# Row maxima moved by DMAs inside SBUF, and causal masking of exponentials on GpSimd

## The chip, the core and the metric

The kernel runs on one core of a Trainium2 chip. The metric is the device time in microseconds (us) of one execution; the number for a kernel is the median of several runs. An execution is also recorded by the hardware profiler, instruction by instruction. The engines are named as the profile names them: PE is the matrix engine (PEld its weight loads), DVE the vector engine, ACT the scalar engine, POOL GpSimd, and SP the engine that here only issues DMAs. PE writes into PSUM, which has eight banks of 512 fp32 columns on each of the 128 partitions; DVE and ACT read PSUM, and POOL in this kernel reads and writes SBUF only.

## The reference, cut to what matters

The reference is a stack of eight gated layers over x (4 batches, 256 tokens, 256 features). The change lies in one of them, the cross-attention of layer 1: 16 heads of 16 features, queries from the normalized x, keys and values from a context of 64 features, and a causal mask. Per batch and head it computes

```
q = (layernorm(x) @ Wq.T), k and v from ctx @ Wkv_expand.T     # 256 x 16 each
scores = (q @ k.T) / sqrt(16), where key index > query index: masked out
attn = softmax(scores, axis=-1)
out = (attn @ v), heads side by side, @ Wout.T
x = x + tanh(g_xattn[1]) * out
```

A softmax is not changed if any constant is taken off all scores of one query. The kernel takes off the maximum of that query's unmasked scores, so that the exponentials stay in range.

## The kernel before, in words

**Layout.** Queries and keys lie transposed: features on partitions, tokens along the row. The sixteen heads are handled in four quadruples j = 0..3; in one quadruple, head n = 0..3 has the 32 partitions 32n to 32n+31, of which 16 are features. Partition 32n+16 (`D1` within the group) is one more row: in the keys tile `kT` it holds 1.0, in the queries tile `qT` it starts as zero. Whatever is written into that row of `qT` is added to every score of that query, so the negated maximum is put there. The 256 x 256 scores of one head have three 128 x 128 blocks that are not wholly masked: two on the diagonal (blocks 0 and 2) and one below it (block 1). They fill 384 columns of a PSUM bank.

**Two passes over the scores.** `Maxima.score(j)` computes the scores with queries on the partitions (lines 945 and 950), reduces each block's row maximum on DVE (line 956), and joins the two blocks of the second half of the queries (lines 961, 962). `Maxima.late(j)`, one round later, turns these columns into rows with two PE transposes (line 968) and DVE adds the transposed 128 x 256 tile to the queries of quadruple j (line 971). For that the maxima are put into column 16 of each 32-wide group of a zeroed tile (`cms`). `Sums.score(j)` then computes the same scores with keys on the partitions (lines 985 and 990), now with the maximum taken off, and ACT takes the exponential of each head's 384 columns (line 996) into the SBUF tile `pT`. `Sums.sum(j)`, one round later, multiplies `pT` with the values (lines 1004 and 1009); a column of ones in the values gives the softmax's denominators.

**The mask** is added by PE: in both passes `masked(side)` first multiplies an identity with a constant tile `cmask` that has -1e30 at the masked places of the two diagonal blocks (line 919, four products of 256 columns, one for each head's bank), and the scores are accumulated on top. `side` chooses the orientation.

**The order of work.** Within this stage the order of PE, DVE, ACT and POOL instructions is the order in which the program gives them; DMAs of SP, and work of later stages, are placed by the scheduler. The stage is a loop of rounds n = 0, 1, 2, ... (line 1071), four for each of the four batches. In round n the quadruple n mod 4 of batch b = n div 4 goes through `Maxima.score`, then the products of the round before (`Sums.sum`), then `Sums.score` for the same quadruple of batch b-1, then one to three steps of an unrelated top-k on DVE (`graph_rows`, lines 511 to 518), then the late parts: `Maxima.late`, `Sums.late` (every second round, PE transposes of line 1025 and DVE work), a turn of the attention output (line 1041), its product with the output weights, and in rounds 1, 5 and 9 the query projection of the next batch (both line 237). Maxima run in rounds 0 to 15, Sums in rounds 4 to 19. All PSUM tiles take one of eight banks in turn: four for a `Maxima.score`, four for a `Sums.score`, one for the accumulated products over two rounds, one for each late transpose.

Of the kernel before, what the change touches and what calls it, by code (L numbers as in the profile page):

```python
# [18 lines left out]
F32 = mybir.dt.float32  # L19
BF16 = mybir.dt.bfloat16  # L20
U32 = mybir.dt.uint32
AF = mybir.ActivationFunctionType
ALU = mybir.AluOpType
AX = mybir.AxisListType
# [3 lines left out]
P = 128  # L28
B, S, D, C = 4, 256, 256, 64
# [5 lines left out]
H1, D1 = 16, 16  # L35
# [8 lines left out]
NEG = -1.0e30  # L44
# [24 lines left out]
def flamingo(ctx: ExitStack, tc: tile.TileContext, a: dict, out: bass.AP):  # L69
    nc = tc.nc  # L70

    const = ctx.enter_context(tc.tile_pool(name="const", bufs=1))
# [18 lines left out]
    def bank(dtype=F32):  # L91
        return pools[1].tile([P, 512 if dtype == F32 else 1024], dtype, tag="b1", name="b1")
# [72 lines left out]
    ident = const.tile([P, P], F32, tag="ident", name="ident")  # L165
# [461 lines left out]
    with tc.tile_pool(name="l0a", bufs=1) as lp:  # L627
        tiles0 = normalized(0, *statistics(0))
        pk = bank()
        for i in range(2):  # L630
            nc.tensor.matmul(
                pk[half(i), :], cw[half(i), CW_KV0 : CW_KV0 + C], ctxT[half(i)].rearrange("c h s -> c (h s)"),
                start=True, stop=True,
            )
        pn = [bank()[:, : 4 * C].rearrange("p (t c) -> p t c", t=4) for _ in range(2)]
# [134 lines left out]
    onesb = const.tile([P, P], BF16, tag="onesb", name="onesb")  # L770
    nc.gpsimd.memset(onesb, 1.0)


    cmask = const.tile([P, 2, 3, P], BF16, tag="cmask", name="cmask")
    nc.gpsimd.memset(cmask, 0.0)
    for side, sign in ((0, -1), (1, 1)):
        for blk in (0, 2):
            nc.gpsimd.affine_select(
                out=cmask[:, side, blk, :], in_=cmask[:, side, blk, :], pattern=[[sign, P]],
                compare_op=ALU.is_ge, fill=NEG, base=0, channel_multiplier=-sign,  # L780
            )

    rows_in = tc.dram_tile([NB * P, D], F32, name="rows_in")
    rows_out = tc.dram_tile([NB * P, D], F32, name="rows_out")
# [4 lines left out]
        out=before, in_=onesb, pattern=[[1, P]], compare_op=ALU.is_ge, fill=0.0, base=-1, channel_multiplier=-1  # L789
# [4 lines left out]
        out=lower, in_=lower, pattern=[[1, E], [-1, E]], compare_op=ALU.is_ge, fill=0.0, base=-1,  # L794
        channel_multiplier=0,
# [102 lines left out]

    with ExitStack():
        lp = l1a
        wo = weights(a["l1_wo"], KC * D)
        nc.sync.dma_start(
            rows_in.rearrange("(n p) d -> p n d", p=P), zero.unsqueeze(1).to_broadcast([P, NB, D])
        )
        cms = []
        for n in range(2):
            cm = lp.tile([P, 2, 4, 32], F32, tag=f"cm1_{n}", name=f"cm1_{n}", bufs=1)
            nc.gpsimd.memset(cm, 0.0)  # L910
            cms.append(cm)
        def group(n):
            return slice(32 * n, 32 * (n + 1))

        def masked(side):

            pn = [bank() for _ in range(4)]
            for n in range(4):
                nc.tensor.matmul(
                    pn[n][:, : 3 * P].rearrange("p (a k) -> p a k", a=3)[:, 0::2, :], identb,  # L920
                    cmask[:, side, 0::2, :], start=True, stop=False,
                )
            return pn

        class Maxima:
# [14 lines left out]

            def score(self, j):
                b, qT = self.b, self.qT
                pn = masked(0)
                for n in range(4):
                    nc.tensor.matmul(
                        pn[n][:, :P], qT[group(n), j, :P], kT[group(n), j, b * S : b * S + P],
                        start=False, stop=True,
                    )
                for n in range(4):
                    nc.tensor.matmul(  # L950
                        pn[n][:, P : 3 * P], qT[group(n), j, P:], kT[group(n), j, b * S : (b + 1) * S],
                        start=False, stop=True, skip_group_check=True,
                    )
                m3 = lp.tile([P, 4, 3], F32, tag="m31", name="m31")
                for n in range(4):
                    nc.vector.tensor_reduce(  # L956
                        m3[:, n, :], pn[n][:, : 3 * P].rearrange("p (a k) -> p a k", a=3), AX.X, ALU.max,
                        negate=True,
                    )
                cm = cms[j % 2]  # L960
                nc.vector.tensor_copy(cm[:, 0, :, D1], m3[:, :, 0])
                nc.vector.tensor_tensor(cm[:, 1, :, D1], m3[:, :, 1], m3[:, :, 2], ALU.min)

            def late(self, j):

                pt = bank()[:, :S]
                for qt in range(2):
                    nc.tensor.transpose(
                        pt[:, qt * P : (qt + 1) * P], cms[j % 2][:, qt].rearrange("p g c -> p (g c)"), ident
                    )  # L970
                nc.vector.tensor_add(self.qT[:, j, :], self.qT[:, j, :], pt)

        class Sums:

# [5 lines left out]

            def score(self, j):
                b, qT = self.b, self.qT
                pn = masked(1)
                for n in range(4):
                    nc.tensor.matmul(
                        pn[n][:, : 2 * P], kT[group(n), j, b * S : b * S + P], qT[group(n), j, :],
                        start=False, stop=True, skip_group_check=True,
                    )
                for n in range(4):
                    nc.tensor.matmul(  # L990
                        pn[n][:, 2 * P : 3 * P], kT[group(n), j, b * S + P : (b + 1) * S], qT[group(n), j, P:],
                        start=False, stop=True,
                    )
                self.pT = lp.tile([P, 4, 3 * P], F32, tag="pT1", name="pT1")
                for n in range(4):
                    nc.scalar.activation(self.pT[:, n, :], pn[n][:, : 3 * P], AF.Exp, scale=0.25)
                return self.pT

            def sum(self, j, pT):
# [60 lines left out]
        with ExitStack():  # L1060
# [10 lines left out]
            for n in range(steps + 5):  # L1071
                b, j = divmod(n, 4)
# [547 lines left out]
```

## Time and profile before

| What | Value |
|---|---|
| median of 6 runs (lowest to highest) | 792.01 us (790.2 to 794.72) |
| the profiled execution's own time | 788.29 us |
| its span in the profile | 786.6 us |
| mean granted TensorE clock | 0.939 |
| first to last score reduction of the stage (line 956) | 127.2 to 206.8 us |
| first to last exponential of the stage (line 996) | 145.7 to 226.4 us |
| PE busy between 165 and 205 us | 39.4 of 40 us |
| POOL busy between 145 and 205 us | 0.04 of 60 us |

All sums below are made against the one profiled execution. Times along the span count from its start. A group of instructions is named by its line in the kernel, its engine and its operation; a mean belongs to one instruction of the group. An fp32 product is recorded as two MATMUL instructions, so that four products of a quadruple appear as eight.

### The profile page before, as it was taken

The page shows a single profiled execution, that of the slowest core. Times are in us where ns is not written, and L with a number is a line of the kernel's source. Part 1 is how long each engine was busy: PE and PEld are TensorE (multiplying, and loading weights), DVE is VectorE, ACT ScalarE, POOL GpSimd, SP SyncE. Part 2 cuts the span into 40 slices and gives each one's busy share as a digit, 9 for nine tenths or more (in the row PEclk, how much of TensorE's full clock was granted, in tenths as well). Part 3 has the DMA queues.
Part 4 walks back from the last instruction along what each step waited for, and adds up shares of the span by engine and source line. Part 5 has one row for each costly group of instructions (what it writes and reads, how often), then busy time and mean ns, then how long its engine had stood idle before and what let it go on. Part 6 is the DMA issues. An engine that isn't in the chain of part 4 may idle for free.

```text
span 786.6 us, 11427 instructions
## 1 busy us (share of the span) xinstructions
PE 701.7 (89%) x4121; PEld 422.6 (54%) x4121; DVE 465.9 (59%) x1321; ACT 329.3 (42%) x685; POOL 192.0 (24%) x264
## 2 busy tenths in 40 slices
PE   6799989799986996897999969999989889979996
PEld 3444445566554765545677456555434244557754
DVE  4687998678868787340243558878757234133324
ACT  3657574543536555420133101565545743023310
POOL 2324382000010012136042731000010012723243
PEclk9779999899999999699899999999979989989999
DMA  7430112100000000015297331000000001379923
GB/s 261 157 118 1 40 41 80 42 2 22 1 21 1 1 1 0 1 48 175 73 340 242 94 137 59 1 2 1 1 1 2 1 1 52 131 257 348 322 91 106
DMA packets 32848, 64.35 MB, mean 82 GB/s; under 512 B 5180, under 2 KB 22488, under 8 KB 32536
## 3 DMA queue, kind: packets, MB, share of 16 engines
q0 software_dynamic: 8224, 31.76, 11.9%
q1 hardware_dynamic: 24136, 31.47, 11.8%
q8 instruction: 33, 0.54, 0.3%
q10 hardware_dynamic: 432, 0.39, 0.2%
q14 instruction: 23, 0.19, 0.1%
HBM read 49.31 MB, written 14.30 MB: 81 GB/s over the span
## 4 chain that ended last, share of the span: by engine, by line
PE 32%; issue 31%; DVE 4%; ACT 4%; DMA 1%; POOL 1%; another core or an unknown queue 0%; SPq 0%; DVEq 0%; POOLq 0%; ACTq 0%
PE b L237 16%; PE b L430 4%; PE b L378 4%; PE b L1174 2%; DVE x L403 2%; PE b L350 1%; PE b L368 1%; PE b L1004 1%; ACT gs L1147 1%; ACT hwork L1185 1%; DMA d_w<-in_ffn_r_dram,d_of 1%; ACT hqT L1198 1%; ACT xn L198 0%; DMA d_x<-rows_in 0%
## 5 line engine op out<-in xcount | busy, mean ns | idle before, releaser
L237 PE MATMUL b<-xnT,w 128*128 128x512 f32 (+2 forms) x288 | 121.0, 578 | 4.6 <-ACT xnT L114 4.6
L1360 DVE TENSOR_REDUCE pad<-b 128x2 f32<-128x512 f32 x128 | 80.9, 684 | 24.6 <-PE b L1384 24.1
L237 PEld LDWEIGHTS b<-xnT,w 128*128 128x128 f32 (+1 forms) x288 | 56.2, 199 | 61.5 <-issue 53.2
L1391 ACT ACTIVATE pT<-b 128x512 f32<-128x512 f32 x128 | 68.6, 598 | 47.6 <-PE b L1384 47.6
L1384 PE MATMUL b<-qm,kT 32*128 32x512 f32 x256 | 75.1, 653 | 1.2 <-ACT pT L1391 1.2
L1353 PE MATMUL b<-kT,qT 32*128 32x256 f32 x512 | 73.3, 427 | 1.7 <-DVE pad L1360 1.7
L343 POOL DMA_INDIRECT d_w<-in_ffn_r_dram,d_of x46 | 43.5, 945 | 99.6 <-PE b L350 72.0
L415 ACT ACTIVATE sil<-b 128x512 f32<-128x512 f32 (+1 forms) x28 | 16.6, 596 | 118.0 <-PE b L237 76.6
L430 PE MATMUL b<-w,hT 128*128 128x256 f32 x224 | 55.6, 400 | 8.4 <-issue 5.8
L817 PE MATMUL b<-w,xnT 128*128 128x512 f32 x128 | 61.1, 633 | 0.0
L237 PE MATMUL b<-d_w,d_xT 128*128 128x256 f32 (+1 forms) x184 | 56.9, 432 | 4.6 <-ACT d_xT L114 1.9
L1353 PEld LDWEIGHTS b<-kT,qT 32*128 32x128 f32 x512 | 43.2, 198 | 31.8 <-issue 10.2
L430 PEld LDWEIGHTS b<-w,hT 128*128 128x128 f32 x224 | 43.0, 197 | 22.2 <-issue 14.0
L416 DVE TENSOR_TENSOR hT<-b,sil 128x512 f32<-128x512 f32 (+1 forms) x28 | 19.3, 689 | 47.0 <-ACT sil L415 38.1
L189 POOL TENSOR_TENSOR ln_rstd<-ln_ve,neghalf 128x4 f32<-128x4 f32 x12 | 12.3, 1026 | 130.8 <-DVE ln_shift L187 130.0
L956 DVE TENSOR_REDUCE m<-b 128x3 f32<-128x384 f32 x64 | 31.2, 549 | 18.8 <-PE b L950 18.6
L817 PEld LDWEIGHTS b<-w,xnT 128*128 128x128 f32 x128 | 25.2, 202 | 31.8 <-issue 31.8
L833 POOL TENSOR_TENSOR re<-re 128x512 f32<-128x512 f32 (+1 forms) x32 | 33.0, 1037 | 30.1 <-ACT re L825 28.9
L395 POOL DMA_INDIRECT d_yt<-rows_out,d_row x32 | 31.0, 968 | 33.4 <-DMA rows_out<-d_y 23.7
L237 PEld LDWEIGHTS b<-d_w,d_xT 128*128 128x128 f32 x184 | 32.0, 194 | 13.1 <-issue 2.7
L378 PE MATMUL b<-d_w,d_hT 88*128 88x256 f32 (+1 forms) x138 | 37.3, 380 | 0.0
L328 POOL DMA_INDIRECT rows_in<-xn,d_row x32 | 31.3, 977 | 24.6 <-DVE d_pick L314 15.1
(287 smaller groups left out, 1263.3 us busy)
## 6 DMA issues: line engine op xcount, KB each, us to landing
d_x<-rows_in SPq DMA_DIRECT2D x46, 128.0 KB
rows_out<-d_y SPq DMA_DIRECT2D x46, 128.0 KB
w<-in_ffn_s_dram SPq DMA_DIRECT2D x13, 384.0 KB
w<-in_l_w_dram SPq DMA_DIRECT2D x6, 512.0 KB
rows_in<-zero SPq DMA_DIRECT2D x1, 2944.0 KB
w<-in_expert_w_dram SPq DMA_DIRECT2D x4, 512.0 KB
x<-in_x_dram SPq DMA_DIRECT2D x8, 128.0 KB
kT<-in_l_kT_dram SPq DMA_DIRECT2D x1, 1024.0 KB
```

The source lines that it names most:

```text
L237: nc.tensor.matmul(dst, lhs(kc), rhs(kc), start=kc == 0, stop=kc == KC - 1)
L328: sent = nc.gpsimd.indirect_dma_start(out=rows_in, out_offset=self.indices(self.at[:, n, t : t + 1]), in_=xn, in_offset=None)
L343: nc.gpsimd.indirect_dma_start(out=w, out_offset=None, in_=src, in_offset=self.indices(self.of[:, n : n + 1]))
L378: nc.tensor.matmul(po, hbT[:hs, c * P : (c + 1) * P], w[:hs, c0 : c0 + D], start=c == 0, stop=c == parts - 1)
L430: nc.tensor.matmul(po, hT[:hs, j, i * P : (i + 1) * P], w[:hs, 4 * hs : 4 * hs + D], start=j == 0, stop=j == len(ws) - 1,)
L817: nc.tensor.matmul(pe, xt[:, kc, i * P : (i + 1) * P], ws0[j][:, kc * 2 * D : (kc + 1) * 2 * D], start=False, stop=kc == KC - 1,)
L833: nc.gpsimd.tensor_add(re[:, :n, :], re[:, :n, :], re[:, n : 2 * n, :])
L956: nc.vector.tensor_reduce(m3[:, n, :], pn[n][:, : 3 * P].rearrange("p (a k) -> p a k", a=3), AX.X, ALU.max, negate=True,)
L1353: nc.tensor.matmul(pn[:, half * S : (half + 1) * S], self.qT[group(k), ah, g0 + half, qt * P : (qt + 1) * P], kT[group(k), ah, self.b * S ...
L1360: nc.vector.tensor_reduce(self.pads[qt][:, ah, g0 : g0 + 2, k, D3], pn.rearrange("p (g s) -> p g s", g=2), AX.X, ALU.max, negate=True,)
L1384: nc.tensor.matmul(pn, kT[group(k), ah, c : c + P], self.qm[group(k), ah, g0 : g0 + 2, :], start=True, stop=True)
L1391: nc.scalar.activation(self.pT[u][:, k, :], pn, AF.Exp, scale=D3**-0.5)
```

## The change: what it does

Three edits, all in this stage:

1. The maxima of two quadruples (an even j and the next) are collected in one tile `max1` of eight columns for each half of the queries. Every second round two PE transposes turn them into eight rows of 256 (not two transposes in every round), ACT copies these rows from PSUM to SBUF (`rows1`), and four DMAs issued by SP write, for head n, the two rows of the two quadruples into partition 32n+16 of `qT`. The DVE additions of line 971, the zeroed tiles `cms` and one of the two DVE joins in two rounds go away.
2. `Sums.score` no longer starts from the mask product; its first products start the bank. The exponentials of masked places are then wrong numbers, and two GpSimd `affine_select` instructions (for blocks 0 and 2, each over four heads, 128 partitions x 512 fp32 elements, in place in `pT`) replace them with zero.
3. `cmask` keeps one orientation, for the maxima's pass, which still adds the mask by PE.

```diff
-    cmask = const.tile([P, 2, 3, P], BF16, tag="cmask", name="cmask")
+    cmask = const.tile([P, 3, P], BF16, tag="cmask", name="cmask")
...
-        cms = []
-        for n in range(2):
-            cm = lp.tile([P, 2, 4, 32], F32, tag=f"cm1_{n}", name=f"cm1_{n}", bufs=1)
-            nc.gpsimd.memset(cm, 0.0)
-            cms.append(cm)
+        def row(n):
+
+            return slice(32 * n + D1, 32 * n + D1 + 1)
...
-                pn = masked(0)
+                pn = masked()
...
-                cm = cms[j % 2]
-                nc.vector.tensor_copy(cm[:, 0, :, D1], m3[:, :, 0])
-                nc.vector.tensor_tensor(cm[:, 1, :, D1], m3[:, :, 1], m3[:, :, 2], ALU.min)
+                if j % 2:
+                    m3 = self.m3
+                    self.max = lp.tile([P, 2, 4, 2], F32, tag="max1", name="max1")
+                    to = [self.max[:, qt].rearrange("p n j -> p j n") for qt in range(2)]
+                    nc.vector.tensor_copy(to[0], m3[:, :, :, 0])
+                    nc.vector.tensor_tensor(to[1], m3[:, :, :, 1], m3[:, :, :, 2], ALU.min)
 
             def late(self, j):
 
+                if j % 2 == 0:
+                    return
                 pt = bank()[:, :S]
                 for qt in range(2):
                     nc.tensor.transpose(
-                        pt[:, qt * P : (qt + 1) * P], cms[j % 2][:, qt].rearrange("p g c -> p (g c)"), ident
-                    )
-                nc.vector.tensor_add(self.qT[:, j, :], self.qT[:, j, :], pt)
+                        pt[:8, qt * P : (qt + 1) * P], self.max[:, qt].rearrange("p n j -> p (n j)"), ident
+                    )
+                rowsT = lp.tile([8, S], F32, tag="rows1", name="rows1")
+                nc.scalar.copy(rowsT, pt[:8])
+                for n in range(4):
+                    nc.sync.dma_start(self.qT[row(n), j - 1 : j + 1, :], rowsT[2 * n : 2 * n + 2, :])
...
-                pn = masked(1)
+                pn = [bank() for _ in range(4)]
                 for n in range(4):
                     nc.tensor.matmul(
                         pn[n][:, : 2 * P], kT[group(n), j, b * S : b * S + P], qT[group(n), j, :],
-                        start=False, stop=True, skip_group_check=True,
+                        start=True, stop=True, skip_group_check=True,
                     )
...
                 for n in range(4):
                     nc.scalar.activation(self.pT[:, n, :], pn[n][:, : 3 * P], AF.Exp, scale=0.25)
+
+                for blk in (0, 2):
+                    diagonal = self.pT[:, :, blk * P : (blk + 1) * P]
+                    nc.gpsimd.affine_select(
+                        out=diagonal, in_=diagonal, pattern=[[0, 4], [1, P]], compare_op=ALU.is_ge, fill=0.0,
+                        base=0, channel_multiplier=-1,
+                    )
                 return self.pT
```

## The prediction, made before the changed kernel ran

> **What bounds the kernel now.** I read the page for the engines first, then busy time by window inside the stage, then the timeline of one round, then POOL's groups by shape. The page:
>
> ```profile
> span 786.6 us, 11427 instructions
> PE   701.7 (89%) x4121; PEld 422.6 (54%) x4121; DVE 465.9 (59%) x1321; ACT 329.3 (42%) x685; POOL 192.0 (24%) x264
> ```
>
> PE is the busiest by far, POOL nearly free. The windows (length, then busy time and instruction count of PE, PEld, DVE, ACT, POOL, then granted clock, DMA share and GB/s) show it in the changed stage:
>
> ```profile
> 159.00:163.00 4.00, 4.00 (x62) 2.75 (x59) 3.66 (x14) 2.11 (x5) 0.00 (x0) 1.00 0.00 0
> 163.00:167.00 4.00, 3.85 (x58) 2.41 (x54) 3.01 (x10) 1.64 (x4) 0.00 (x0) 1.00 0.02 4
> 207.00:211.00 4.00, 2.58 (x21) 1.25 (x22) 3.90 (x18) 3.96 (x10) 0.00 (x0) 1.00 0.00 0
> ```
>
> PE is full in the rounds that run both passes, so work taken from PE should count there; at 207 us PE is not full, and ACT is. But a full PE also covers a chain. The timeline of the round from 163.62 us (start, length, engine, line):
>
> ```profile
> 163.62 0.71 PE L985 MATMUL b<-qT,kT 32*128 32x256 f32 x8
> 164.16 0.40 PE L990 MATMUL b<-qT,kT 32*128 32x128 f32 x8
> 164.49 0.44 PE L968 MATMUL b<-ident,cm 128*128 128x128 f32 x2
> 164.64 1.64 ACT L996 ACTIVATE pT<-b 128x384 f32<-128x384 f32 x4 [2.69 <-PE b L990]
> 164.76 1.06 PE L919 MATMUL b<-cmask,identb 128*128 128x256 bf16 x4
> 165.38 0.41 DVE L971 TENSOR_TENSOR qT<-qT,b 128x256 f32<-128x256 f32 x1
> 165.76 0.31 PEld L945 LDWEIGHTS b<-kT,qT 32*128 32x128 f32 x8 [0.48 <-issue]
> 166.63 0.64 PE L1004 MATMUL b<-pT,va 128*32 128x256 f32 x8
> 167.08 0.40 PE L1009 MATMUL b<-pT,va 128*32 128x128 f32 x8
> 167.42 0.61 PE L919 MATMUL b<-cmask,identb 128*128 128x256 bf16 x4
> ```
>
> The loop is: Sums' scores (985, 990), exponentials until 166.28, products (1004, 1009) from 166.63, mask products, next scores at 167.96. The exponentials end only 0.35 us before PE comes to 1004: other PE work just covers them. Whatever is put between exponentials and products has 0.35 us of cover per round. The change puts two POOL instructions there. POOL's rows by shape:
>
> ```profile
> L833 POOL TENSOR_TENSOR re<-re 128x512 f32<-128x512 f32 x16 | 21.0, 1310 | 28.9 <-ACT re L825 28.9
> L1347 POOL COPY pad<-xn 128x128 f32<-128x128 f32 x16 | 4.3, 288 | 30.2 <-PE b L1324 24.4 <-issue 5.8
> L778 POOL TENSOR_SCALAR_AFFINE_SELECT cmask<-cmask 128x128 bf16<-128x128 bf16 x4 | 1.0, 292 | 0.1
> L1115 POOL COPY had<-had 128x256 f32<-128x256 f32 x1 | 0.4, 393 | 21.1 <-PE b L1009 21.1
> L793 POOL TENSOR_SCALAR_AFFINE_SELECT lower<-lower 128x64 f32<-128x64 f32 x1 | 0.3, 290 | 0.1
> ```
>
> **The price of one select, S.** No row has 512 elements. Copies of 128 and 256 columns take 288 and 393 ns, 0.82 ns an element; from the 128-column select (283 ns in fp32, 292 in bf16) that gives 0.283 + 384 x 0.82 ns = 0.60 us. The two-input rows (763 ns at 256 columns, 1310 at 512: 2.14 ns an element) give 1.10. The select over 64 elements in 8 runs costs as much as 128 in one, so a run costs about 10 ns, and with POOL's smallest start (132 ns, one-column iota) the select's own rate is at most (283 - 132)/128 = 1.2 ns: 0.78 us with its four runs. Between 0.63 and 0.78 I take S = 0.70; 0.60 and 1.10 stay as ends. [...]
>
> **The loop after the change**, from the first exponential of a round to that of the next: exponentials 1.64; ACT to POOL 0.08 (line 825's end to line 833's start); two selects 2S - 0.04 (neighbouring selects start 0.04 before the last one's end); POOL to PE 0.06 (ACT to PE at 208.73 took 0.05); 1004 waits for the first select only and runs beside the second; 1009 to the next PE group 0.33 (167.08 to 167.41); 985 to the end of 990 0.94; PE to ACT 0.08. That is 3.09 + 2S = 4.49 us. Now it is 4.33. PE's own work shrinks by 0.54 for the four mask products (167.42 to 167.96) and 0.17 for the transposes in odd rounds (164.49 to 164.66), so where PE has more than this loop to do, it gains that.
>
> **The sum, round by round**, from the starts of the exponentials in ACT's timeline (145.68, 150.78, 160.30, 164.64, 168.97, 173.30, 181.14, 187.22, 191.55, 195.89, 200.99, 208.26, 212.17, 216.18, 220.19, 224.75 for rounds 4 to 19):
> - Rounds 0 to 4, maxima alone: DVE is the limit from 135 to 145 us (3.9 of 4 busy); PE waits there 2.39 for the reductions and 0.99 for the addition of 971. Two additions (0.41 each) and a join (0.33) leave DVE's path, and the transposes that PE waited 0.62 for at 129.83. ACT's table load (143.41, 1.28 long) is the next limit. Gain 1.2 (0 to 2).
> - 4 to 5: 5.10, PE waiting for banks at half clock; taken as 4.6: -0.5 (0 to -0.6).
> - 5 to 6 and 9 to 10, with query projections: PE-bound, -0.7 each. 10 to 11, with the output product: -0.54. 13 to 14, with the turn: 5.10 to 4.49, -0.6.
> - 6 to 9 and 11 to 13, five plain rounds: 4.33 to 4.49, +0.75 together.
> - 14 to 15: 7.27, set by the next stage's layer norm (DVE statistics, POOL power 1.01, four ACT rows of line 198); only 971 leaves DVE's way, -0.4.
> - 15 to 16: 3.91 to 4.49, +0.57. 16 to 18: 4.01 to 4.49 twice, +0.95. 18 to 19: 4.56 to 4.49, -0.07. These rounds have no maxima's pass, so PE has nothing to cover the selects with.
> - After the last exponentials: 2.53 to the end of 1009 (224.75 to 227.28) becomes 2.14 + 2S = 3.54, +1.01; the next stage's first instructions wait for that 1009 (POOL's line 1115 in the fence above).
>
> Together -1.4 us. Every 0.1 us on S costs 2.2, since eleven of these intervals carry two selects.
>
> **Edits costed otherwise.** The DMAs: 32 of 2 KB. SP needs about 0.3 for each (0.27 for the small ones at 22 us), and a small write took 2.8 from issue to landing (SP's wait for `eb_parts`). Copied by ACT (0.38, as line 114 at 128x256) about 2.1 after the end of 990, four issued by 3.3, landed by 6.1; the rows are read two rounds later, at about 8. So hidden by 1.9; if not, each exposed microsecond is paid up to eight times. SP's queue also carries ten hoisted weight loads, some waiting up to 54.5 us for a buffer; the rows would have to be queued ahead of those. ACT's copy runs while ACT waits for PE anyway (2.69 idle): nothing, else 8 x 0.38. The products of 985 now carry both the wait for a bank and that for a DMA; extra PE waits cost 0.05 each (event semaphores at line 968): between 0 and 8 x 4 x 0.05 = 1.6, I take +0.6, as about three of eight pairs begin in loop-bound rounds. POOL's memsets and two fewer selects lie in idle POOL time: nothing. [...]
>
> The sum is -1.4 + 0.6 = **-0.8 us**: 787.5 against the profiled 788.29, and by the same difference 791.2 against the median of 792.01, which lies 3.7 above the profiled run.
>
> **Rivals.**
> 1. *Slower: the selects cost more than the small rows say.* Place: between the last exponential and 1004/1009, in eleven intervals. For it: POOL's two-input rate and a tensor_scalar of 128 columns (line 1117) that took 609 ns. Against: the select itself takes 283 at that size. At S = 1.10 it is 0.4 x 22 = 8.8 worse, 800. It decides from S = 0.74 (even) and by more than the bound below from 0.85.
> 2. *1004 waits for both selects*, if the dependency is not kept per block. Then its 0.46 lies in the loop ten times: +4.6, 795.8. For: they write one tile. Against: 1004 shows that exponentials are tracked per head (it starts 0.05 after the first of them at 208.78).
> 3. *The rows land late*, behind weight loads in SP's queue (0.22 of the DMA engines' time at 179 to 183): 1 us in four to eight rounds, 795 to 799.
> 4. *PE stays the limit*, the selects being nearer the 283 ns row, or DVE's relief in the first rounds larger. At S = 0.3 the loop is 3.7, PE's own need 3.63: -9, 782.
>
> **How the numbers follow.** The runs of this kernel can tell about 0.3%, 2.4 us, from no change. Forecast (S 0.60 to 0.80, nothing else): 0.46, own range 788.5 to 793.5, of which 0.14 is faster by that and 0.32 within. Rival 1: 0.22 (0.21 slower, 0.01 within). Rival 2: 0.10 (0.08, 0.02). Rival 3: 0.10 (0.08, 0.02). Rival 4: 0.12, faster. Sums: faster 0.26, same 0.37, slower 0.37. The range 786 to 798 leaves out the deep half of rival 4 and the far part of rivals 1 and 3, about 2 in 10.
>
> **What would show it.** POOL gets 32 selects of 0.6 to 0.8 us. In plain rounds 1004 waits for POOL, and the distance of the exponentials is 4.4 to 4.6; in rounds 16 to 19 too. Around the projections it is 0.7 shorter than now. Reductions of round 4 begin about 1 us earlier against the first. PE's busy share falls. I am wrong if a select takes over 0.85, if 985 waits for a DMA, if ACT or POOL places the next stage's layer norm between exponentials and selects, or if plain rounds fall to 3.7.

## The result, and the profile after

| | before | after |
|---|---|---|
| median | 791.75 us | 796.03 us (790.5 to 799.85) |
| the profiled execution's own time, its span | 788.29, 786.6 | 790.12, 788.4 |
| mean granted TensorE clock of that execution | 0.939 | 0.932 |

The ratio is 1.0048, with a 95% interval of 1.0031 to 1.0066: slower by about 4 us, where 0.8 us less was forecast. The forecast range (786 to 798) holds the time. A second profile of the changed kernel has a span of 794.4 us at a clock of 0.928; where the two differ, both are given.

The page of the changed kernel, its totals:

```profile
span 788.4 us, 11383 instructions
PE 690.9 (88%) x4041; PEld 416.8 (53%) x4041; DVE 458.4 (58%) x1289; ACT 331.0 (42%) x693; POOL 210.8 (27%) x292
```

PE is busy for 10.8 us less and the span is 1.8 us longer. The new POOL group, from the page's groups (busy us, mean ns of one, idle before), and the waits that it causes, from the view of waits (us in total, times, longest):

```profile
L1008 POOL TENSOR_SCALAR_AFFINE_SELECT pT<-pT 128x512 f32<-128x512 f32 x32 | 19.8, 642 | 66.5 <-ACT pT L1004 66.5
```

```profile
POOL pT L1008 <- ACT pT L1004: 66.5, 16, 7.8
PEld b L1019 <- POOL pT L1008: 16.4, 11, 4.1
PE b L1019 <- POOL pT L1008: 12.2, 9, 3.9
```

A select takes 0.64 us. PE waits 12.2 us in all for selects, and one of these nine waits is 3.9 us long. The timeline shows first a plain round, then round 15 with that wait. In the new numbering 993 and 998 are Sums' scores (985 and 990 before), 1004 the exponentials (996), 1008 the selects, 1019 and 1024 the products (1004 and 1009), 918, 944 and 949 the mask and scores of the maxima's pass.

```profile
164.52 1.64 ACT L1004 ACTIVATE pT<-b 128x384 f32<-128x384 f32 x4 [0.31 <-PE b L998]
...
165.14 0.60 PE L918 MATMUL b<-cmask,identb 128*128 128x256 bf16 x4
...
165.99 0.61 PE L949 MATMUL b<-kT,qT 32*128 32x256 f32 x8
166.02 0.34 ACT L977 COPY rows<-b 8x256 f32<-8x256 f32 x1
166.29 1.22 POOL L1008 TENSOR_SCALAR_AFFINE_SELECT pT<-pT 128x512 f32<-128x512 f32 x2 [3.21 <-ACT pT L1004]
166.39 2.51 SPq L979 DMA_DIRECT2D qT<-rows  x4
...
166.98 0.64 PE L1019 MATMUL b<-pT,va 128*32 128x256 f32 x8 [0.37 <-POOL pT L1008]
...
200.01 2.07 ACT L198 ACTIVATE xn<-x,ln_shift,ln_rstd 128x256 f32<-128x256 f32 x4 [2.53 <-POOL ln_shift L190]
...
201.99 1.59 ACT L1004 ACTIVATE pT<-b 128x384 f32<-128x384 f32 x4
...
203.66 1.23 POOL L1008 TENSOR_SCALAR_AFFINE_SELECT pT<-pT 128x512 f32<-128x512 f32 x2 [3.68 <-ACT pT L1004]
...
204.36 1.08 PE L1019 MATMUL b<-pT,va 128*32 128x256 f32 x8 [3.88 <-POOL pT L1008]
```

In the plain round the chain is as forecast: exponentials to 166.16, the first select to about 166.93, the products from 166.98, beside the second select. In round 15 the scores were done at 200.48, but ACT was by then in the next stage's layer norm (line 198, four rows, to 202.08); the exponentials come behind it, and the selects behind them. PE stands for 3.88 us. In before the same layer norm stood in the same place:

```profile
206.28 2.08 ACT L198 ACTIVATE xn<-x,ln_shift,ln_rstd 128x256 f32<-128x256 f32 x4 [3.65 <-POOL ln_shift L190]
208.26 1.59 ACT L996 ACTIVATE pT<-b 128x384 f32<-128x384 f32 x4
208.78 1.53 PE L1004 MATMUL b<-pT,va 128*32 128x256 f32 x7 [1.42 <-ACT pT L996]
```

PE waited only 1.42 us there, because its first product could start 0.52 us after the first exponential began; now it waits for all four heads' exponentials and a select. And the products that follow take 1.08 us where the plain round's took 0.64. The windows (busy time and count of PE, PEld, DVE, ACT and POOL, then granted clock, DMA share, GB/s) say why; after the first line they are cut every 3.41 us, for a reason given in the last section:

```profile
163.00:167.00 4.00, 3.63 (x58) 2.51 (x54) 2.68 (x9) 2.43 (x6) 0.79 (x3) 1.00 0.00 0
...
196.74:200.15 3.41, 3.41 (x55) 2.42 (x57) 3.24 (x13) 0.50 (x2) 2.33 (x4) 1.00 0.01 2
200.15:203.56 3.41, 0.33 (x12) 0.14 (x4) 3.41 (x14) 3.41 (x8) 0.00 (x0) 1.00 0.00 1
203.56:206.97 3.41, 2.61 (x28) 1.57 (x32) 2.30 (x12) 1.99 (x6) 1.23 (x2) 0.50 0.00 0
206.97:210.39 3.42, 2.38 (x26) 1.35 (x18) 1.45 (x6) 2.07 (x6) 1.21 (x2) 0.50 0.02 5
210.39:213.80 3.41, 3.41 (x36) 2.28 (x28) 3.17 (x11) 0.44 (x2) 0.01 (x1) 0.50 0.01 2
213.80:217.22 3.42, 1.43 (x22) 0.62 (x24) 1.51 (x5) 1.91 (x7) 1.38 (x2) 1.00 0.01 2
217.22:220.63 3.41, 3.41 (x21) 2.83 (x15) 0.07 (x1) 2.05 (x5) 0.45 (x1) 0.50 0.00 0
```

After the wait the granted clock is half for 10.2 us, and again for 3.4 us from 217.2 and from 227.5. In before it is 1.00 from 149 to 228 us. With half the clock the products take 1.08 instead of 0.64 and the scores of 993 take 1.24 instead of 0.71, and both lie on the path of these rounds. The next table follows the time: starts of the exponentials, as differences to before, in us.

| interval | before | forecast change | change, first profile | second profile |
|---|---|---|---|---|
| first reduction to round 4 | 18.53 | -1.2 | -2.50 | -2.50 |
| 4 to 5 | 5.10 | -0.5 | -0.18 | +0.10 |
| 5 to 6, 9 to 10 | 17.36 | -1.4 | -1.36 | -1.35 |
| 10 to 11, 13 to 14 | 11.18 | -1.14 | -1.14 | -1.20 |
| five plain rounds | 21.67 | +0.75 | +0.50 | +0.48 |
| 14 to 15 | 7.27 | -0.4 | -0.14 | -0.23 |
| 15 to 19 | 16.49 | +1.45 | +5.21 | +3.75 |
| last exponentials to the end of the products | 2.53 | +1.01 | +0.94 | +1.35 |
| sum | 100.13 | -1.4 | +1.3 | +0.4 |

At round 15 the changed kernel leads by 6.3 us (201.99 against 208.26), of which 1.45 lie ahead of the stage (first reduction at 125.70 against 127.15; in the second profile it is at 127.51). At the end of the stage's products the lead is 0.1 us (227.16 against 227.28). In the next stage it falls behind: the first product of line 278 (at 340.0 us in before) starts 212.9 us after the first reduction in before, 215.1 and 216.7 in the two profiles after. Between 228 and 272 us the clock is half for about 10 and 16 us, against 3 in before.

### The profile page after: what moved, and what is told of

Its sections match the earlier page's. It is cut to its first block, busy times and chain, and to the rows that moved or that the text cites. A ratio compares the mean times of both kernels' runs of the same rounds, so it can differ in the third digit from the quotient of the medians.

```text
span 788.4 us, 11383 instructions
## 1 busy us (share of the span) xinstructions
PE 690.9 (88%) x4041; PEld 416.8 (53%) x4041; DVE 458.4 (58%) x1289; ACT 331.0 (42%) x693; POOL 210.8 (27%) x292
## 4 chain that ended last, share of the span: by engine, by line
PE 40%; issue 31%; DVE 11%; ACT 9%; DMA 4%; POOL 3%; another core or an unknown queue 1%; SPq 1%; POOLq 0%; ACTq 0%; DVEq 0%
PE b L237 18%; PE b L430 4%; PE b L378 3%; PE b L815 3%; PE b L1189 3%; ACT pT L1004 2%; DVE x L403 2%; ACT xn L198 2%; PE b L993 1%; PE b L1019 1%; DMA d_w<-in_ffn_r_dram,d_of 1%; PE b L350 1%; DVE g_work L514 1%; DVE g_m L511 1%; PE b L368 1%
## 5 line engine op out<-in xcount | busy, mean ns | idle before, releaser
L237 PE MATMUL b<-xnT,w 128*128 128x512 f32 (+2 forms) x288 | 119.2, 571 | 4.8 <-ACT xnT L114 4.8
L1008 POOL TENSOR_SCALAR_AFFINE_SELECT pT<-pT 128x512 f32<-128x512 f32 x32 | 19.8, 642 | 66.5 <-ACT pT L1004 66.5
```

What stands on the lines that cost most here:

```text
L237: nc.tensor.matmul(dst, lhs(kc), rhs(kc), start=kc == 0, stop=kc == KC - 1)
```

## Experiments

The questions were which half of the change costs, whether the late loss is the clock or the chain through the selects, what takes the clock down, and what the select's length is worth. Every run below was timed against the kernel before on its own chip.

**One half each.** In the first kernel the maxima go through the DMAs but PE masks both passes and there is no select; in the second the selects replace the mask product but the maxima are transposed and added as before.

```diff
-                pn = [bank() for _ in range(4)]
+                pn = masked(1)
...
-                        start=True, stop=True, skip_group_check=True,
+                        start=False, stop=True, skip_group_check=True,
...
-                for blk in (0, 2):
-                    diagonal = self.pT[:, :, blk * P : (blk + 1) * P]
-                    nc.gpsimd.affine_select(
...
```

The diff is that of the first, against the changed kernel (`cmask` and `masked` have both orientations again). The second is the kernel before with the changed `Sums.score` and a `cmask` of one orientation.

> The changed maxima (pairs, ACT copy, DMAs) alone; both masks stay products on PE. My terms for this part: 1.2 to 2.5 us off the first rounds, 0.17 on PE in odd rounds, nothing lost: ratio 0.995 to 0.998 by both theories, and the clock in rounds 15 to 19 as in the kernel before (1.0). If the rows land late, 985 waits for a DMA and the ratio is over 1.

> The selects and no mask product for the sums' scores alone; maxima turned and added by PE and DVE as before. Theory A (clock): the same wait in round 15 and half clock after it, ratio 1.006 to 1.010. Theory B (latency without clock): plain rounds 4.43, rounds 16 to 19 4.43, clock 1.0 there: ratio 1.000 to 1.003.

The maxima alone: 0.9957 (0.9935 to 0.9979), within the band expected. The selects alone: 1.0046 (1.0020 to 1.0073), below the 1.006 to 1.010 expected for the clock and as large as the whole loss, with the same 3.88 us wait in round 15 and the same half clock, as the windows of that run show:

```profile
204.25:207.66 3.41, 0.52 (x4) 0.20 (x2) 3.23 (x15) 3.35 (x8) 0.02 (x1) 1.00 0.00 0
207.66:211.07 3.41, 2.42 (x24) 1.41 (x28) 3.24 (x13) 2.51 (x6) 1.23 (x2) 0.50 0.00 0
211.07:214.49 3.42, 2.48 (x22) 1.69 (x18) 1.62 (x8) 1.64 (x4) 1.02 (x2) 0.50 0.03 7
```

So the first half is a gain of some 3.4 us and the second a loss of some 3.6. Added up they would cancel (1.0003, uncertain by about 0.35% to each side by the two intervals); together in the changed kernel they lose 0.3 to 0.5%. That the first half's gain is not kept beside the second is therefore likely, and not shown.

**The clock.** The first kernel keeps the change whole and adds PE products that nothing reads (their results are unused): 12 in round 15 behind the scores, 6 in rounds 16, 17 and 19. If the loss is the clock, they bring time back although they are more work.

```diff
+                if sums is not None and n >= 15:
+                    warm = bank()
+                    for _ in range(12 if n == 15 else 0 if n == 18 else 6):
+                        nc.tensor.matmul(warm, onesb, wq1[0][:, :512], start=True, stop=True)
                 graph_rows(0 if n < 4 else 1 if n < 16 else 3)
```

> The changed kernel with filler products on PE (12 of 128x512 bf16 after Sums.score in round 15, 6 in rounds 16, 17 and 19; their results are not used). Theory A (granted clock): in the changed kernel PE waits 3.88 us in round 15 and the clock falls to half from 205 to 216 us and at times later; the fillers keep PE busy in that wait, the clock stays at 1.0, rounds 16 to 19 take 4.4 to 4.6 instead of 5.0 to 5.9, and the kernel is 4 to 6 us faster than the changed one: ratio to the kernel before 0.995 to 0.999. Theory B (the selects' latency alone): rounds 16 to 19 stay above 5, ratio 1.004 to 1.008.

0.9979 (0.9955 to 1.0003), timed beside the selects alone at 1.0046. Rounds 15 to 19 take 5.09, 4.65, 4.43 and 4.43 us in place of 5.48, 5.89, 5.05 and 5.28, and the clock holds to 227. The control puts the same products into the kernel before:

> The kernel before with the same products of no use as warm15 (12 in round 15, 6 in rounds 16, 17 and 19; their results are read by nothing). A control: warm15 shows the clock only if the products do nothing by themselves. The kernel before already keeps its clock at 1.0 through rounds 15 to 19. Theory A (the products help by the clock alone): ratio 1.000 to 1.004, distances in rounds 15 to 19 as in before (3.91, 4.01, 4.01, 4.56) or up to 0.2 us longer where PE is late. Rival C (the products change something else, such as the order on the queues): a ratio of 0.997 or less.

1.0031 (1.0011 to 1.0050): by themselves they cost time (16 to 17 takes 4.31 us in place of 4.01, a little more than expected). So work that costs 0.3% where the clock is whole brings the changed kernel from between 1.0027 and 1.0048 (three values, that of its second half alone among them) to 0.9979, a gain of 0.5 to 0.7%; against the lowest of the three the intervals just touch. By the rounds' own times (18.60 us with the products, 21.70 and 20.24 without, 16.49 in before) the clock is 3.1 and 1.6 us of the 5.2 and 3.8 lost in rounds 15 to 19. Next, is it the one long wait alone? Here the products stand in round 15 only:

```diff
-                    for _ in range(12 if n == 15 else 0 if n == 18 else 6):
+                    for _ in range(12 if n == 15 else 0):
```

> The changed kernel with 12 filler products on PE in round 15 only (results not used). Theory A1: the one wait of 3.88 us in round 15 trips the clock; without it the clock stays 1.0 to the end of the stage although rounds 16 to 19 have their selects and no filler: rounds of 4.4 to 4.7, ratio 0.996 to 1.000. Theory A2: the thin PE work of rounds 16 to 19 behind the selects drops the clock by itself: half clock in some of 208 to 226 us, rounds over 5, ratio over 1.002.

1.0045 (1.0020 to 1.0070): nothing is won. The clock gets through round 15, and then falls in round 16:

```profile
203.86:207.28 3.42, 2.29 (x34) 1.25 (x34) 2.12 (x11) 2.15 (x6) 1.15 (x2) 1.00 0.02 5
207.28:210.69 3.41, 1.75 (x24) 0.89 (x28) 2.48 (x9) 1.76 (x6) 1.23 (x2) 1.00 0.00 1
210.69:214.10 3.41, 2.45 (x20) 1.71 (x20) 3.17 (x10) 1.63 (x5) 0.00 (x0) 0.50 0.02 4
```

In 207.28 to 210.69 PE waits 1.58 us for round 16's select and is busy for half of the stretch; the next stretch is at half clock. The long wait is one cause; the selects leave PE so little to do in rounds 16 to 19 (1.75 of 3.41 us in that stretch), where no maxima's pass fills the waits, that the clock falls there too.

**No selects where nothing covers them.** From round 15 on PE masks the scores, as in before; rounds 4 to 14 keep the selects.

```diff
-                pn = [bank() for _ in range(4)]
+                by_pe = 4 * (b + 1) + j >= 15
+                pn = masked(1) if by_pe else [bank() for _ in range(4)]
...
-                for blk in (0, 2):
+                if not by_pe:
+                    for blk in (0, 2):
...
```

> The changed kernel, but from round 15 on the sums' scores are masked by PE products as before, with no selects; rounds 4 to 14 keep the selects. Theory A (clock): the wait in round 15 falls by about 1.3 to 2.6 us, below what drops the clock; rounds 16 to 18 return to 3.9 to 4.1, ratio 0.991 to 0.996. Theory B (latency): the same rounds return to about 4.0 at whatever clock, a gain of about 3 over the changed kernel, ratio 1.000 to 1.002.

0.9943 (0.9918 to 0.9969), 789.03 us: faster than before, with a clock of 1.00 throughout the last rounds. Against the maxima alone (0.9957) the intervals overlap: the selects in rounds 4 to 14 are worth nothing that these runs can tell. Their plain rounds take 4.43 us where those with PE's mask take 4.01 and 4.33 by turns, and the rounds with projections are 0.5 us shorter, which about balances.

In this kernel and in that with the maxima alone 15 to 16 takes 5.00 us, against 3.91 in before, at full clock and without any select there. ACT's timeline of the run with the maxima alone shows the cause:

```profile
203.81 1.60 ACT L1006 ACTIVATE pT<-b 128x384 f32<-128x384 f32 x4
206.72 0.91 ACT L1246 ACTIVATE xn<-xn,q_s 128x256 f32<-128x256 f32 x2 [1.32 <-DVE q_s L1238]
207.54 0.56 ACT L114 COPY oT<-b 128x512 f32<-128x512 f32 x1
208.00 0.91 ACT L1246 ACTIVATE xn<-xn,q_s 128x256 f32<-128x256 f32 x2
208.81 1.61 ACT L1006 ACTIVATE pT<-b 128x384 f32<-128x384 f32 x4
```

ACT takes four rows of the next stage's quantization between the two rounds' exponentials, and now waits 1.32 us for DVE's scale of them (in before these rows followed the exponentials at once, at 209.89). DVE finishes this scale 2.73 us after the last row of ACT's layer norm (at 206.63), in before 1.43 us after it (209.79): it now does two more steps of the top-k before the scale than in before (lines 511 and 514). So DVE's order has changed there; why is not shown.

**The length of the selects.** Doubled, and cut in two or in four, each time with PE masking from round 15 on so that the last rounds are out of it. The cut of a select goes by heads, so that the first may start when two exponentials are done, not four. The doubled one issues the same two selects twice; the diff is that of the cut in two, and in four it is `h` in `range(4)` with 128 x 128 each.

```diff
-                for blk in (0, 2):
-                    diagonal = self.pT[:, :, blk * P : (blk + 1) * P]
+                for h in (0, 2):
+                    for blk in (0, 2):
+                        diagonal = self.pT[:, h : h + 2, blk * P : (blk + 1) * P]
```

> The kernel with selects in rounds 4 to 14 and PE's mask from round 15, each select issued twice (the second changes nothing). By my loop each round that is bound by it grows by 1.22 us (one select 0.64, less 0.04 overlap, twice): plain rounds 4.43 to 5.65, six or seven such intervals: 7 to 10 us over the run with single selects, ratio to the kernel before 1.003 to 1.007. If PE or DVE bound those rounds and the selects lay beside them, the ratio stays under 0.998. [...]

> The same kernel with each select cut into one for heads 0 and 1 and one for heads 2 and 3 (128 x 256 elements), so that half of them run beside the last two exponentials. A select of 256 should take 0.40 (between 0.283 at 128 and 0.642 at 512). By the loop 0.8 instead of 1.3 is left behind the last exponential: plain rounds 3.95 to 4.05, ratio 0.989 to 0.993. If PE is the limit of plain rounds at 4.43, no change from 0.994.

> PE's mask from round 15, and in rounds 4 to 14 one pair of selects for each head (eight of 128 x 128, 0.28 each). By the loop only the last head's pair lies behind the last exponential (0.6 instead of 0.8): plain rounds 3.8. But eight selects of 0.28 take 2.1 against 1.64 of exponentials, so POOL may fall behind and leave 0.9: then 4.0 to 4.1 as with four. Ratio 0.990 to 0.993; PE's own need (3.6) would show as PE without waits in plain rounds.

| selects in each of the rounds 4 to 14 | mean ns of one | plain round, us | ratio |
|---|---|---|---|
| four of 128 x 512 (doubled) | 634 | 5.54 | 1.0105 (1.0077 to 1.0134) |
| two of 128 x 512 | 635 | 4.43 | 0.9943 (0.9918 to 0.9969) |
| four of 128 x 256 | 412 | 3.99 | 0.9920 (0.9890 to 0.9950) |
| eight of 128 x 128 | 298 | 4.22 | 0.9968 (0.9944 to 0.9992) |

Doubling adds 1.11 us to a plain round, where two more selects take 1.2; two of its rounds take 6.51 and 6.77 with a half clock, and the loss (12.8 us over the uncut one by the ratios) is beyond the 7 to 10 expected. Cut in two, the first half of the selects lies under the exponentials: the four begin 1.00 us after the first exponential begins and end 0.85 us after the last one ends, where the uncut ones end 1.35 us after it. Cut in four, POOL begins sooner (0.56 us after the first) but its eight selects take 2.06 us in place of 1.49 and end 0.98 us after the last exponential; the plain round is longer again, and longer than the 4.0 to 4.1 expected. The plain rounds tell the three apart; of the ratios, those of one piece and of two have overlapping intervals, and so have, barely, those of two and of four.

**The change with its selects cut in two, in all rounds**, and nothing else:

> The changed kernel with selects in all rounds, each cut in two (heads 0 and 1, heads 2 and 3). By the loop, plain rounds 3.99 as in the run with selects cut to rounds 4 to 14, rounds 16 to 19 about 4.0, and the wait of round 15 falls from 3.88 to about 3.4. Theory A2 (thin PE work drops the clock): PE works as little as in the changed kernel but waits 0.45 less per round. If that is enough to hold the clock, ratio 0.992 to 0.996; if the clock still falls after 204 us, rounds 16 to 19 take 4.6 to 5.5 and the ratio is 0.998 to 1.003.

0.9926 (0.9904 to 0.9948), 787.86 us: faster than before with all of the change kept. POOL's group and the windows of round 15 and after:

```profile
L1009 POOL TENSOR_SCALAR_AFFINE_SELECT pT<-pT 128x256 f32<-128x256 f32 x64 | 24.1, 410 | 54.3 <-ACT pT L1004 54.3
```

```profile
197.38:200.79 3.41, 0.98 (x21) 0.72 (x16) 3.41 (x13) 2.90 (x7) 0.40 (x3) 1.00 0.00 1
200.79:204.20 3.41, 2.95 (x24) 1.57 (x28) 2.94 (x15) 2.00 (x6) 1.51 (x4) 0.50 0.00 0
204.20:207.62 3.42, 2.41 (x36) 1.32 (x30) 2.00 (x7) 2.59 (x8) 1.52 (x4) 1.00 0.02 5
207.62:211.03 3.41, 2.15 (x30) 1.34 (x26) 3.19 (x11) 1.83 (x6) 0.83 (x3) 1.00 0.02 5
```

The selects cost POOL more in sum (24.1 against 19.8 us) and the path less. PE's wait in round 15 is 2.89 us; one stretch of 3.41 us is at half clock, and rounds 15 to 19 take 5.09, 4.24, 3.99 and 4.03. Whether the remaining stretch is worth filling:

> The changed kernel with each select cut in two of 128x256, and the products of warm15 besides (their results are read by nothing). In the run of the cut selects alone the clock dips only in 200 to 204 (0.60) and rounds 15 to 19 take 5.09, 4.24, 3.99, 4.03. Theory A2 (the clock falls where PE has thin work behind the selects; with shorter selects little of that is left): ratio 0.990 to 0.994 as there (0.9926), rounds 16 to 19 unchanged within 0.2 us. If the clock still costs much in that kernel, the ratio would be 0.988 or less.

0.9946 (0.9925 to 0.9967): the unused products bring nothing more. The value lies just above the expected band; the interval covers it. With them the clock is 1.00 throughout these rounds, and they take 5.08, 4.25, 3.98 and 4.04, as without them: the one stretch at half clock cost no time there.

**The changed kernel again**, for a second profile:

> The changed kernel itself, for a second profile: its profiled execution was 6 us below the median of its runs. Theory A: this profile, near 795, has half clock from about 204 to 216 us again, and more half clock behind it than the first one; PE's waits and the order are the same. Theory B: the same clock, and the extra time lies in waits or DMAs of later stages.

1.0027 (1.0001 to 1.0053), with the same wait (3.87 us) and half clock after it; its stretches fall differently (3.4 us from 206.3 and from 216.5, 6.8 from 226.8), and the rounds with them (5.48, 4.66, 5.66, 4.43).

## Why the prediction was wrong

**Right: the select.** 0.64 us, within 0.63 to 0.78 though at its lower end (0.70 taken). The copies' rate gave the near bound; rival 1 (0.85 and more) fell. The loop by its own terms is 3.09 + 2 x 0.64 = 4.37, measured 4.43 in plain rounds; most of the rest is the step from ACT to POOL, 0.13 for the 0.08 taken. Selects that took longer were rare: 31 of the 32 took 632 to 643 ns. One took 788 ns; its pair ran for 1.38 us from 215.13, and DVE's line 518 for 0.48 from 214.94. In the run with the products in round 15 only the longest took 865 ns; of the cut ones single selects took 647 and 651 where the median is 407, and 471 where it is 294. In before, one of POOL's eight instructions of line 834 took 1.05 us (from 103.04, beside DVE's line 602); their median is 0.73. That DVE's instructions are the cause is not shown.

**Right: the dependency, the rows and the covers.** 1019 starts after the first select, so rival 2 fell. No product waits for the rows' DMAs, so rival 3 fell, although four issues on SP's queue take 2.51 us in the record and not 1.2. The 2.8 us taken from issue to landing was a misreading: it is SP's wait alone, and SP's last issue of those writes ended at 17.76 us and the wait at 22.39, 4.6 later; so the margin was thinner than the 1.9 us worked out. Nor does the +0.6 for extra PE waits show: the plain rounds take 4.43 to 4.44 in both profiles, whether they begin a pair or not. The rounds with projections, the output product and the turn came out within 0.2 us each. PE did not stay the limit in plain rounds (rival 4).

**Off in size: the first rounds.** The gain to round 4 is 2.5 us, not 1.2, and beyond its bounds of 0 to 2 (all of it comes with the maxima: 16.03 us in the run with them alone, 17.82 with the selects alone, 18.53 in before); 4 to 5 gives less than the 0.5 in return. Together -2.7 and -2.4 against -1.7.

**Wrong: the steps "15 to 16: 3.91 to 4.49", "16 to 18" and "18 to 19".** They price 15 to 19 at 17.96 us; it takes 21.70 and 20.24. Two things were left out. First, these four rounds take 18.60 with the clock held at 1.0 (the run with the unused products): 0.6 above the forecast, nearly all of it in 15 to 16, which is set by ACT's quantization rows waiting for DVE and takes 5.00 even without selects. The prediction named ACT's layer norm between exponentials and selects as a sign of being wrong; that did not happen, the rows stand between the exponentials of two rounds, and the step had no price for them. Second, and larger, the chain was worked out with every product at full clock. The step that says that PE "has nothing to cover the selects with" in these rounds stopped there: it counted the wait and not that the clock could halve behind it (in the first profile PE is busy for 0.33 us of 200.15 to 203.56, and the next three stretches of 3.41 us are at 0.50). By the times above, the clock is 3.1 us in one profile and 1.6 in the other, in these rounds alone.

**Missing: anything after the stage.** The sum ended with 1009. The profiles show half clock for about 6 and 12 us more than before between 228 and 272 us, and a loss against before that has grown to 2.2 and 3.8 us at line 278. How much of the 4 us lies inside the stage and how much behind it differs between the two profiles and is not settled; with the unused products, all in rounds 15 to 19, the loss at line 278 is 0.7 us and the kernel is not slower, which shows where it starts.

**The chances.** Slower had 0.37, made of selects that cost too much, a dependency on both selects and late rows. None of these happened; the kernel became slower by a way that no rival named. That the range up to 798 holds the time is luck: its upper part was there for those rivals.

## What to carry to other kernels

When work moves from a full engine to an idle one that stands in series, ask in each round what the first engine does meanwhile, and if it is PE, how busy it stays: here the clock halved after waits of 1.58 to 3.88 us, and a round's products then took 1.08 us in place of 0.64. Cut such an operation along the axis in which its inputs arrive, so that it starts under them. Here two pieces in all rounds won 1.0 to 1.2% over one, most of it from round 15 on: with PE's mask there, one piece and two cannot be told apart by the ratio. Four pieces lost part of the plain round's gain again (4.22 us against 3.99). And end the sum a stage later than the edit.

## What the runs showed of the hardware

In each of the seven runs named below, from about 152 to 275 us, the granted clock changes only at points that lie whole multiples of 3.41 us apart. In rounds 15 to 19 of the changed kernel's two profiles the falls from full to half lie 13.66 and 10.24 us apart, and 10.24 and 10.24; that is 4, 3, 3 and 3 times 3.41 us, and stretches at half clock last 3.4, 6.8 or 10.2 us. Cut at these points, the windows of seven runs (the two of the changed kernel, the selects alone, the products in round 15 only and in 15 to 19, the doubled and the cut selects), from about 152 us for 36 stretches each, came out as follows. PE busy for at most 0.51 of a stretch at full clock: the next was at half clock, 27 times of 29. Busy for 0.53 or more: the next was at full clock, 179 times of 179. At half clock, after 0.86 or more came the full clock (27 of 27), and after 0.85 or less it did not (10 of 10). Both exceptions (0.46 and 0.51) are in the run with doubled selects. Outside this part of the span these shares do not divide as well. In the first profile of the changed kernel PE is busy for 0.59, 0.90 and 0.74 of the stretches from 138.7, 333.3 and 490.3 us at full clock, and the next is at half; from 39.7 us it is busy throughout at half clock, and the next is at half too. In before, which is not among the seven, 0.43 from 250.4 us is followed by full clock. So PE's busy share is not all that decides.

The run with the unused products in rounds 15 to 19 has the same edge at its end:

```profile
203.56:206.97 3.41, 2.24 (x14) 0.91 (x16) 3.41 (x18) 2.52 (x7) 0.82 (x2) 1.00 0.00 0
...
224.04:227.45 3.41, 1.55 (x20) 0.51 (x19) 0.76 (x3) 1.27 (x3) 2.02 (x5) 1.00 0.00 0
227.45:230.86 3.41, 3.41 (x17) 3.40 (x17) 2.08 (x8) 0.74 (x2) 0.48 (x1) 0.50 0.00 0
```

At 0.66 (2.24 of 3.41) the clock holds, at 0.45 it falls. It fits these counts that a wait of 1.58 us cost the clock in one kernel and one of 1.56 in the kernel with cut selects did not: the first lay within one stretch (207.28 to 210.69), the second across two (the point at 217.86 divides it). It fits too that the two profiles of one kernel lose it in different places: round 15's wait of 3.88 us ends 0.80 us after such a point in the first (204.36, 203.56), and that of 3.87 at 0.01 in the second (206.28, 206.27). These shares are read from traces whose ends of products are modelled; no run was made to test the edge by itself.
